# A ConvNeXt block with a gated head on one core: the first stage's ScalarE and VectorE order kept as written, centering products spread out, first image's GELUs placed behind evacuations

## The chip, the cores and the metric

The kernel runs on one core of one Trainium2 chip. The metric is the device time of one execution in microseconds (us). Engines are named as in the profile: PE is TensorE's matmul, PEld its weight load, DVE is VectorE, ACT is ScalarE, POOL is GpSimd, and SP is SyncE, which here only issues DMAs.

## The reference

The input x has 32 images of 384 channels and 28 x 28 pixels, in float32. One ConvNeXt-V2 block is followed by a gate on each image:

```python
y = conv7x7_depthwise(x)                      # 384 channels, padding 3
y = layernorm_over_channels(y) * ln_g + ln_b  # eps 1e-6
y = gelu(y @ w1 + b1)                         # 384 -> 1536
gx = sqrt(sum(y * y over the pixels))         # of each image and channel
y = grn_g * (y * gx / (mean(gx) + 1e-6)) + grn_b + y
y = x + (y @ w2 + b2)                         # 1536 -> 384, back to NCHW
# gate: mean, max and min over the pixels of y go through small matrices
out = sigmoid(logits[:, :, None, None] + y)
```

## The kernel before, in words

**The first stage** (0 to about 525 us) does the depthwise convolution and the layer norm's statistics for all images at once. It runs over NK = 48 steps `s` of TC = 8 channels, each step over 4 pairs `c2` of channels. `conv` makes three products of each channel with a banded matrix `tmat` (L661, L663, L665) into a PSUM bank `pc`. DVE then transposes the pair into `yt` (L668) and adds it to `acc` (L676), ACT squares it into `sq` (L681), and POOL adds two pairs' squares to `ssum` (L686). At the end of a step `yt` is stored to `yd`. Every 4 steps use one block `xt` of 32 channels. The next block is made meanwhile by `spread`: for each of 8 groups, `pad_x` copies an input tile into `xpad` (on ACT after the first block, L471), and `turn_x` transposes it on PE in two halves (L483) into a bank `pt`, which DVE (first half, L492) or ACT (second half, L494) copies into `xt`. The pad of group i+1 is issued at the first half of group i.

The weights are made in the same stage. `center_w` folds the layer norm's scale, shift and mean into w1 with small products (L566 into `pb`, L577 into `pm`) and three DVE updates for each `pm` (L583). `form_w` makes 15 combinations of w1 blocks (`UPSTEPS`, from step U1) and 38 of w2 blocks (`STEPS`, from step U2) for a fast matrix product. A form begins on POOL (L549) if two of its terms can be joined with a plain sum or difference, else on ACT (L552), and goes on on POOL (L555). Its tile `u` is one of three; the SP queue stores it to `u1d` or `u2d` at the end of the next step, after that step's `yd` store (L832).

The last two steps run in two halves of the images, so that the first image can be read back early. `first_image` adds the bias to it and makes its feature combinations (`forms_up`, L356). `finish` turns the sums into the factors of the layer norm, which go through DRAM (`rsd`) to `rb`.

**The second stage** runs image by image. `up(b)` is the first matrix product: two halves of 30 products each (L914) into banks A, B and C; ACT copies a bank (L921) or DVE adds it (L923 to L931). `down(b)` is the second one (L1042), whose operands POOL sums first (`sums`, L1003). Between them stand GELU (L879), the sum of squares (L890), `grn` (L938 to L950) and `scale` (L322, L324). For image 0 the layer norm's factor is multiplied after the product (`stretch`, L884, on POOL for the first six slices, on DVE and POOL in turn for the others). `within(b)` holds a table of hooks: `at((2, 4 * m), ...)` runs a function after product 4m of the second half of `up(b)`. The order of calls at the start is up(0), up(1), down(0), up(2), down(1), and so on.

**What sets the order on an engine.** The program is traced in Python, and a planner then orders each engine's instructions by its own estimate of when each is ready. `tc.keep_in_program_order(ins)`, here `keep`, ties an instruction to the earlier kept ones of its engine, so that these run as written; the others the planner may place before or after. Before the change, the conv products, the transposes on PE, and DVE's `L668` and `L676` are kept, and so are POOL's feature combinations and sums. Not kept are ACT's squares, pads, copies of `pt`, form copies, bank copies and GELUs, DVE's copies of `pt`, and the stretches.

Of the kernel before, what the change touches and what calls it, by code (L numbers as in the profile page):

```python
# [46 lines left out]
SQ = 4  # L47
# [150 lines left out]
def convnext_gate_kernel(  # L198
# [161 lines left out]
    with ExitStack() as one:  # L360
# [5 lines left out]
        psc = one.enter_context(tc.tile_pool(name="psc", bufs=5, space=bass.MemoryType.PSUM))  # L366
# [97 lines left out]

        def pad_x(i):
# [7 lines left out]
        keep = tc.keep_in_program_order  # L473

        def turn_x(i, h, xt, eng=nc.vector):
# [15 lines left out]
            if eng is nc.vector:  # L491
                eng.tensor_copy(dst, src)  # L492
            else:
                eng.activation(dst, src, AF.Identity)  # L494
# [8 lines left out]
        U1, U2 = 10, 23  # L503
# [38 lines left out]
        def form_w(name, wv, text, dst):  # L542
# [8 lines left out]
            else:  # L551
                nc.scalar.activation(t, blks[0][1], AF.Identity, scale=float(blks[0][0]))  # L552
# [5 lines left out]
        def center_w(part):  # L558

            if part == 0:  # L560
                nc.vector.tensor_copy(lr[:, :, 0], lnb_t)
                nc.vector.tensor_scalar(lr[:, :, 1], lng_t, -1.0 / C, None, ALU.mult)
                pb = psx.tile([P, 4, P], F32, tag="pt", name="pb").rearrange("p a b -> p (a b)")
                for f in range(FB):
                    for cb in range(CB):
                        nc.tensor.matmul(  # L566
                            pb[:, 2 * f : 2 * f + 2], w1r[:, cb, f * P : (f + 1) * P],
                            lr[:, cb], start=(cb == 0), stop=(cb == CB - 1),
                        )
                pbv = pb[:, : 2 * FB].rearrange("p (f v) -> p f v", v=2)  # L570
                nc.vector.tensor_tensor(b1f, pbv[:, :, 0], b1_t, ALU.add)
                nc.vector.tensor_copy(mcol, pbv[:, :, 1])
                return
            f0 = (part - 1) * 4
            pm = psx.tile([P, 4, P], F32, tag="pt", name=f"pm_{part}")
            for i in range(4):
                nc.tensor.matmul(  # L577
                    pm[:, i], mcol[:, f0 + i : f0 + i + 1].to_broadcast([P, P]), ident,
                    start=True, stop=True,
                )  # L580
            for cb in range(CB):
                w = w1r[:, cb, f0 * P : (f0 + 4) * P]
# [54 lines left out]
        def conv(s, c2, yt, xt, b0, b1):  # L637
# [42 lines left out]
            for ci in range(2):  # L680
                nc.scalar.activation(  # L681
                    part(sq)[:, cy % SQ + ci], part(pc[:, :, :N])[:, ci], AF.Square,
                    bias=dwb[:, cc + ci : cc + ci + 1], scale=1.0,
# [48 lines left out]
        def first_image(part):  # L732
# [4 lines left out]
            def raw(eng, cb, q0, q1):  # L737
# [5 lines left out]
                else:  # L743
                    eng.activation(d, src, AF.Identity, bias=dwb_t[:, cb : cb + 1], scale=1.0)
# [11 lines left out]
        for s in range(NK):  # L756
# [8 lines left out]
            if s in later:  # L765
# [3 lines left out]
                nc.gpsimd.tensor_copy(first, xpad[s % NPAD][: dst.shape[0], 0, :1])  # L769
# [6 lines left out]
            if s == NK - 1:  # L776
                y2 = yt, new_yt("yt_a1")
                first_image(0)
                for i in range(5):
# [26 lines left out]
                first_image(1)  # L806
# [70 lines left out]
    def gelu(b, f):  # L877
        y = ys[b][:, f, :]
        nc.scalar.activation(y, y, AF.Gelu, bias=b1f[:, f : f + 1], scale=1.0)  # L879

    def stretch(f, eng):

        y = ys[0][:, f, :].rearrange("p (r w) -> p r w", w=HW)
        eng.tensor_tensor(y, y, rows(rbs[0]), ALU.mult)  # L884
# [374 lines left out]
```

## Time and profile before

| | |
|---|---|
| median of 3 runs | 3081.61 us (3078.28 to 3082.94) |
| the profiled execution | 3081.39 us, its span 3079.6 us |
| busy share of the span | PE 98%, PEld 79%, DVE 64%, ACT 59%, POOL 79% |
| mean granted TensorE clock | 0.991 |
| first stage, PE | last conv product at about 525 us |
| up(0), first product of L914 | 527.6 us |

In the lines of the profile, `L681` is line 681 of the kernel. A line of the instructions in order of time has the start, the duration, the engine, the line and operation, out<-in with shapes, a count of instructions merged into it, and in brackets the idle time ahead of it and what ended that. A float32 product appears as two records. A line of busy time by stretch has the stretch, its length, then PE, PEld, DVE, ACT and POOL busy (with instructions), the granted clock, the DMA engines' share and GB/s. A line of waits has the waiting engine, its tile and line, then the one it waited for, and the total, the times and the longest.

### The profile page before, as it was taken

How to read it: one execution, taken by the hardware profiler on the slowest of the kernel's cores; microseconds unless marked ns; L12 is line 12 of the kernel's file. 1: busy time of each engine (PE TensorE's matmuls, PEld its weight loads, DVE VectorE, ACT ScalarE, POOL GpSimd, SP SyncE). 2: the span in 40 equal slices, each digit the busy share in tenths (PEclk: the TensorE clock that was granted, in tenths of full speed). 3: DMA queues.
4: the chain of work that ended last, by engine and by line, in shares of the span. 5: the costliest groups of instructions: out<-in, count | busy, mean ns of one | idle time of the engine just before them, and what ended most of it. 6: DMA issues, size and time to landing. Idle time of an engine off the chain costs nothing.

```text
span 3079.6 us, 44014 instructions
## 1 busy us (share of the span) xinstructions
PE 3013.7 (98%) x14435; PEld 2437.3 (79%) x14435; DVE 1985.0 (64%) x4555; ACT 1802.5 (59%) x3004; POOL 2438.4 (79%) x1829
## 2 busy tenths in 40 slices
PE   8999999899999999999999999999999999999998
PEld 7999988477777777777777777777777777777777
DVE  4555556656666666666666666666666666666666
ACT  4455554546666666666666666666666666666661
POOL 3356866398888888888888888888888888888897
PEclk9899999999999999999999999999999999999999
DMA  9799897456666666666666666666666666666546
GB/s 358 279 356 349 325 358 252 157 165 197 198 199 203 200 204 203 199 199 197 198 199 198 196 201 200 199 200 202 200 200 202 200 200 202 201 201 202 194 153 201
DMA packets 288475, 673.23 MB, mean 219 GB/s; under 512 B 31199, under 2 KB 111610, under 8 KB 282234
## 3 DMA queue, kind: packets, MB, share of 16 engines
q1 hardware_dynamic: 275156, 631.62, 62.4%
q10 hardware_dynamic: 13094, 38.80, 3.3%
q8 instruction: 118, 1.93, 0.3%
q14 instruction: 107, 0.88, 0.1%
HBM read 575.57 MB, written 94.76 MB: 218 GB/s over the span
## 4 chain that ended last, share of the span: by engine, by line
PE 87%; POOL 7%; DVE 3%; issue 1%; ACT 1%; DMA 1%; ACTq 0%; SPq 0%; DVEq 0%; POOLq 0%
PE ph_C L914 13%; PE ph_A L914 12%; PE ph_B L914 11%; PE pz_A L1042 7%; PE pz_C L1042 7%; PE pz_D L1042 7%; PE pz_F L1042 6%; PE pc L661 5%; PE pc L663 4%; PE pc L665 4%; POOL d_room L1003 3%; PE pt L483 2%; PE pz_H L1042 2%; PE pz_E L1042 2%; PE pz_I L1042 2%; DVE room L315 2%
## 5 line engine op out<-in xcount | busy, mean ns | idle before, releaser
L324 ACT ACTIVATE y<-y,fv,gsc 128x784 f32<-128x784 f32 x372 | 359.1, 1031 | 464.5 <-DVE gsc L950 464.5
L1003 POOL TENSOR_TENSOR d_room<-y 128x588 f32<-128x588 f32 x253 | 364.4, 1441 | 291.4 <-PE pz_B L1042 195.5
L879 ACT ACTIVATE y<-y,b1f 128x784 f32<-128x784 f32 x384 | 350.1, 945 | 230.5 <-DVE y L929 180.2
L914 PE MATMUL ph_A<-room,ws 128*128 128x392 f32 x1240 | 462.3, 495 | 10.6 <-ACT te L921 4.9
L914 PE MATMUL ph_C<-room,ws 128*128 128x392 f32 x1240 | 463.8, 496 | 5.3 <-DVE y L927 3.0
L914 PE MATMUL ph_B<-room,ws 128*128 128x392 f32 x1240 | 463.3, 496 | 5.7 <-ACT y L921 3.5
L1003 POOL TENSOR_TENSOR d_room<-d_room,y 128x588 f32<-128x588 f32 x308 | 440.9, 1436 | 16.8
L914 PEld LDWEIGHTS ph_C<-room,ws 128*128 128x128 f32 x1240 | 234.4, 191 | 190.4 <-DVE y L927 28.6
L914 PEld LDWEIGHTS ph_A<-room,ws 128*128 128x128 f32 x1240 | 236.2, 191 | 185.7 <-ACT te L921 5.6
L914 PEld LDWEIGHTS ph_B<-room,ws 128*128 128x128 f32 x1240 | 236.2, 191 | 171.9 <-ACT y L921 4.6
L890 ACT ACTIVATE junk<-y 128x784 f32<-128x784 f32 x384 | 329.0, 857 | 8.9
L1003 POOL TENSOR_TENSOR d_room<-y,d_room 128x588 f32<-128x588 f32 x214 | 306.2, 1437 | 26.9 <-PE pz_D L1042 15.8
L686 POOL TENSOR_TENSOR ssum<-ssum,sq 128x896 f32<-128x896 f32 (+1 forms) x100 | 201.7, 2017 | 150.6 <-ACT sq L681 148.7
L356 POOL TENSOR_TENSOR room<-room 128x392 f32<-128x392 f32 x303 | 303.5, 1018 | 11.9
L1003 POOL TENSOR_TENSOR y<-y 128x588 f32<-128x588 f32 x180 | 258.7, 1437 | 7.1
L925 DVE TENSOR_TENSOR y<-y,ph_B 128x392 f32<-128x392 f32 x256 | 137.5, 556 | 167.2 <-ACT y L879 123.5
L923 DVE TENSOR_TENSOR y<-y,ph_C 128x392 f32<-128x392 f32 x384 | 212.1, 560 | 26.3 <-PE ph_C L914 1.6
L661 PE MATMUL pc<-xt,tmat 128*128 128x224 f32 x736 | 203.5, 358 | 15.4 <-ACT sq L681 10.1
L1042 PE MATMUL pz_A<-d_room,u 128*128 128x196 f32 x1050 | 202.9, 329 | 0.1
L1042 PEld LDWEIGHTS pz_A<-d_room,u 128*128 128x128 f32 x1050 | 178.8, 190 | 7.7 <-POOL d_room L1003 0.4
L663 PE MATMUL pc<-xt,tmat 128*96 128x192 f32 x736 | 181.7, 329 | 0.0
L665 PE MATMUL pc<-xt,tmat 128*128 128x192 f32 x736 | 181.2, 328 | 0.0
(265 smaller groups left out, 6258.4 us busy)
## 6 DMA issues: line engine op xcount, KB each, us to landing
u<-u2d SPq DMA_DIRECT2D x487, 384.0 KB, 3.8
ws<-u1d SPq DMA_DIRECT2D x384, 320.0 KB, 3.0
tmat<-fs SPq DMA_DIRECT2D x47, 1420.0 KB, 10.5
ws<-u2d SPq DMA_DIRECT2D x121, 384.0 KB, 3.8
yi<-yd SPq DMA_DIRECT2D x95, 448.0 KB, 6.2
yd<-yt SPq DMA_DIRECT2D x46, 896.0 KB, 9.3
x<-in_x SPq DMA_DIRECT2D x32, 1176.0 KB, 5.6
out<-x ACTq DMA_DIRECT2D x31, 1176.0 KB, 9.4
```

Of the source, the lines that this page charges most:

```text
L324: eng.activation(out, in_, AF.Identity, bias=add, scale=mul)
L356: tc.keep_in_program_order(eng.tensor_tensor(d, o[in0], o[in1], op))
L661: keep(nc.tensor.matmul(po, t[:, c, P : 2 * P], xc, start=True, stop=False))
L663: nc.tensor.matmul(lo, t[:, c, 2 * P : T0 + MW], after, start=False, stop=False)
L665: keep(nc.tensor.matmul(hi, t[:, c, :P], before, start=False, stop=True))
L686: nc.gpsimd.tensor_tensor(part(ssum), part(ssum), part(sq), ALU.add)
L879: nc.scalar.activation(y, y, AF.Gelu, bias=b1f[:, f : f + 1], scale=1.0)
L890: nc.scalar.activation(junk, ys[b][:, f, :], AF.Square, accum_out=ssqs[b][:, f : f + 1])
L914: nc.tensor.matmul(banks[t, bk][:, :NH], wts[t][:, i % UG, :], o[opnd], start=(first == 1), stop=True, skip_group_check=True,)
L923: nc.vector.tensor_tensor(d, d, p, ALU.add)
L1003: nc.gpsimd.tensor_tensor(d[0], o[a][0], o[c][0], ALU.add if sign == "+" else ALU.subtract)
L1042: nc.tensor.matmul(pz[:, :NQ4], wt[:, i % UD, t, :], o[opnd][0][:, t, :], start=(first and t == 0), stop=(t == KD - 1), skip_group_check=True,
```

## The change

There are six edits. On ACT and DVE, every instruction of the first stage's loop is now kept: pads, copies of `pt`, squares, form copies, and the first image's bias on ACT. The centering products are no longer made in blocks at the ends of steps 7, 8 and 9; one or two groups follow each pair's conv products in steps 7 to 10, in a PSUM bank of their own (`psb`), and `psc` has four banks instead of five. U1 goes from 10 to 11, the forms of w1 are spread over 9 steps at 3/5 steps each, and those of w2 end one step earlier. `first_image` is in three parts, the first two at the ends of steps 44 and 45 instead of at the start of the last step. POOL's small copies that hold back a load until its step read `acc` instead of `xpad`. In the second stage, image 0's GELUs, squares and stretches and the bank copies of images 0 and 1 are kept, and some hooks move.

```diff
-        psc = one.enter_context(tc.tile_pool(name="psc", bufs=5, space=bass.MemoryType.PSUM))
+        psb = one.enter_context(tc.tile_pool(name="psb", bufs=1, space=bass.MemoryType.PSUM))
+        psc = one.enter_context(tc.tile_pool(name="psc", bufs=4, space=bass.MemoryType.PSUM))
...
             if i < NG:
                 nc.gpsimd.tensor_copy(dst, src)
             else:
-                nc.scalar.activation(dst, src, AF.Identity)
+                keep(nc.scalar.activation(dst, src, AF.Identity))
...
             if eng is nc.vector:
-                eng.tensor_copy(dst, src)
+                keep(eng.tensor_copy(dst, src))
             else:
-                eng.activation(dst, src, AF.Identity)
+                keep(eng.activation(dst, src, AF.Identity))
...
-        U1, U2 = 10, 23
+        U1, U2 = 11, 23
...
-                nc.scalar.activation(t, blks[0][1], AF.Identity, scale=float(blks[0][0]))
+                keep(nc.scalar.activation(t, blks[0][1], AF.Identity, scale=float(blks[0][0])))
...
+        def center_w(n):
+
+            if n < FB:
+                if n == 0:
...
+                    cent["pb"] = psb.tile([P, 4, P], F32, tag="pb", name="pb").rearrange(
+                        "p a b -> p (a b)"
+                    )
+                pb = cent["pb"]
+                for cb in range(CB):
+                    keep(
                         nc.tensor.matmul(
-                            pb[:, 2 * f : 2 * f + 2], w1r[:, cb, f * P : (f + 1) * P],
+                            pb[:, 2 * n : 2 * n + 2], w1r[:, cb, n * P : (n + 1) * P],
                             lr[:, cb], start=(cb == 0), stop=(cb == CB - 1),
                         )
...
+            f = n - FB
+            if f % 4 == 0:
+                cent["pm"] = psb.tile([P, 4, P], F32, tag="pb", name=f"pm_{f}")
+            pm = cent["pm"]
+            keep(
                 nc.tensor.matmul(
-                    pm[:, i], mcol[:, f0 + i : f0 + i + 1].to_broadcast([P, P]), ident,
+                    pm[:, f % 4], mcol[:, f : f + 1].to_broadcast([P, P]), ident,
                     start=True, stop=True,
                 )
+            )
+            if f % 4 < 3:
+                return
             for cb in range(CB):
...
             for ci in range(2):
-                nc.scalar.activation(
-                    part(sq)[:, cy % SQ + ci], part(pc[:, :, :N])[:, ci], AF.Square,
-                    bias=dwb[:, cc + ci : cc + ci + 1], scale=1.0,
+                keep(
+                    nc.scalar.activation(
+                        part(sq)[:, cy % SQ + ci], part(pc[:, :, :N])[:, ci], AF.Square,
+                        bias=dwb[:, cc + ci : cc + ci + 1], scale=1.0,
+                    )
                 )
...
                 raw(nc.scalar, 0, 0, NQD)
                 raw(nc.scalar, 1, 0, NQD)
+            elif part == 1:
                 forms_up(0, nc.gpsimd, early=True)
...
-                nc.gpsimd.tensor_copy(first, xpad[s % NPAD][: dst.shape[0], 0, :1])
+                nc.gpsimd.tensor_copy(first, acc[: dst.shape[0], 0, :1])
...
-                first_image(0)
-                for i in range(5):
+                for i in range(4):
...
-                first_image(1)
+                first_image(2)
...
                     conv(s, c2, yt, xt, 0, B)
+                    q = (s - U1 + 4) * PAIRS + c2
+                    if 0 <= q < 4 * PAIRS:
+                        for n in range(q * 3 // 2, (q + 1) * 3 // 2):
+                            center_w(n)
                     if k + 1 < NX:
                         spread(k + 1, si * PAIRS + c2, xn)
...
+                if NK - 4 <= s:
+                    first_image(s - NK + 4)
...
-            if U1 - 3 <= s < U1:
-                for part in ((0,), (1,), (2, 3))[s - U1 + 3]:
-                    center_w(part)
...
-                if s != U1 + i * 2 // 3:
+                if s != U1 + i * 3 // 5:
...
-                if s != U2 + i * (NK - 2 - U2) // ND:
+                if s != U2 + i * (NK - 3 - U2) // ND:
...
-        nc.scalar.activation(y, y, AF.Gelu, bias=b1f[:, f : f + 1], scale=1.0)
+        ins = nc.scalar.activation(y, y, AF.Gelu, bias=b1f[:, f : f + 1], scale=1.0)
+        if b == 0:
+            tc.keep_in_program_order(ins)
...
-        eng.tensor_tensor(y, y, rows(rbs[0]), ALU.mult)
+        tc.keep_in_program_order(eng.tensor_tensor(y, y, rows(rbs[0]), ALU.mult))
...
-                            nc.scalar.activation(d, p, AF.Identity)
+                            ins = nc.scalar.activation(d, p, AF.Identity)
+                            if b < 2:
+                                tc.keep_in_program_order(ins)
...
-                at((0, 24), normed, 1)
-                at((2, 0), forms_up, 1)
+                at((0, 20), normed, 1)
+                at((0, 24), forms_up, 1)
...
-                at((0, 2 + 2 * m), gelu, p, HF + m)
-                at((0, 14 + m), square, p, HF + m)
-            at((0, 20), grn, p)
+                at((0, 6 + 2 * m), gelu, p, HF + m)
+                at((0, 17 + m), square, p, HF + m)
+            at((0, 23), grn, p)
             for i, f in enumerate(order):
-                at((0, 22) if i < 6 else (2, 0), scale, p, f, V if i % 3 else A)
-            at((0, 23), sums, p)
+                at((0, 24) if i < 6 else (2, 0), scale, p, f, V if i % 3 else A)
+            at((0, 26), sums, p)
...
-                at((2, 2 + 4 * m), gelu, b, m)
+                at((2, (2 if b else 8) + 4 * m), gelu, b, m)
             for m in range(squared(b)):
-                at((2, 28 if m >= HF // 2 else 22 + 2 * m), square, b, m)
+                at((2, 29 if m >= HF // 2 or not b else 22 + 2 * m), square, b, m)
```

More of the change, by code (lines that the diff above doesn't have):

```diff
@@ L463, in load_x @@
             )
+        keep = tc.keep_in_program_order
         def pad_x(i):
@@ L470, in pad_x @@
             else:
-                nc.scalar.activation(dst, src, AF.Identity)
-        keep = tc.keep_in_program_order
+                keep(nc.scalar.activation(dst, src, AF.Identity))
         def turn_x(i, h, xt, eng=nc.vector):
@@ L556, in form_w @@
             stores.append((dst, t))
[L558 to L565, printed above, removed]
+        cent = {}
+        def center_w(n):
+            if n < FB:
+                if n == 0:
+                    nc.vector.tensor_copy(lr[:, :, 0], lnb_t)
+                    nc.vector.tensor_scalar(lr[:, :, 1], lng_t, -1.0 / C, None, ALU.mult)
+                    cent["pb"] = psb.tile([P, 4, P], F32, tag="pb", name="pb").rearrange(
[4 more added lines that the diff above has]
+                    keep(
@@ L566, in center_w @@
                         nc.tensor.matmul(
-                            pb[:, 2 * f : 2 * f + 2], w1r[:, cb, f * P : (f + 1) * P],
+                            pb[:, 2 * n : 2 * n + 2], w1r[:, cb, n * P : (n + 1) * P],
                             lr[:, cb], start=(cb == 0), stop=(cb == CB - 1),
                         )
-                pbv = pb[:, : 2 * FB].rearrange("p (f v) -> p f v", v=2)
-                nc.vector.tensor_tensor(b1f, pbv[:, :, 0], b1_t, ALU.add)
-                nc.vector.tensor_copy(mcol, pbv[:, :, 1])
@@ L573, in center_w @@
-                return
-            f0 = (part - 1) * 4
-            pm = psx.tile([P, 4, P], F32, tag="pt", name=f"pm_{part}")
-            for i in range(4):
+                    )
+                if n == FB - 1:
+                    pbv = pb[:, : 2 * FB].rearrange("p (f v) -> p f v", v=2)
+                    nc.vector.tensor_tensor(b1f, pbv[:, :, 0], b1_t, ALU.add)
+                    nc.vector.tensor_copy(mcol, pbv[:, :, 1])
+                return
+            f = n - FB
+            if f % 4 == 0:
+                cent["pm"] = psb.tile([P, 4, P], F32, tag="pb", name=f"pm_{f}")
@@ L577, in center_w @@
+            pm = cent["pm"]
+            keep(
                 nc.tensor.matmul(
-                    pm[:, i], mcol[:, f0 + i : f0 + i + 1].to_broadcast([P, P]), ident,
+                    pm[:, f % 4], mcol[:, f : f + 1].to_broadcast([P, P]), ident,
                     start=True, stop=True,
                 )
+            )
+            if f % 4 < 3:
+                return
             for cb in range(CB):
-                w = w1r[:, cb, f0 * P : (f0 + 4) * P]
+                w = w1r[:, cb, (f - 3) * P : (f + 1) * P]
@@ L680, in conv @@
             for ci in range(2):
-                nc.scalar.activation(
-                    part(sq)[:, cy % SQ + ci], part(pc[:, :, :N])[:, ci], AF.Square,
-                    bias=dwb[:, cc + ci : cc + ci + 1], scale=1.0,
+                keep(
+                    nc.scalar.activation(
+                        part(sq)[:, cy % SQ + ci], part(pc[:, :, :N])[:, ci], AF.Square,
+                        bias=dwb[:, cc + ci : cc + ci + 1], scale=1.0,
+                    )
                 )
@@ L743, in raw @@
                 else:
-                    eng.activation(d, src, AF.Identity, bias=dwb_t[:, cb : cb + 1], scale=1.0)
+                    keep(
+                        eng.activation(d, src, AF.Identity, bias=dwb_t[:, cb : cb + 1], scale=1.0)
+                    )
             if part == 0:
@@ L889, in square @@
         junk = junkp.tile([P, NT], F32, tag="junk", name=f"junk_{b}_{f}")
-        nc.scalar.activation(junk, ys[b][:, f, :], AF.Square, accum_out=ssqs[b][:, f : f + 1])
+        ins = nc.scalar.activation(
+            junk, ys[b][:, f, :], AF.Square, accum_out=ssqs[b][:, f : f + 1]
+        )
+        if b == 0:
+            tc.keep_in_program_order(ins)
     def up(b, hooks):
@@ L920, in up @@
                         if how == "copy":
-                            nc.scalar.activation(d, p, AF.Identity)
+                            ins = nc.scalar.activation(d, p, AF.Identity)
+                            if b < 2:
+                                tc.keep_in_program_order(ins)
                         elif how == "add":
```

## The prediction

> **What bounds the kernel now.** I read the page first: TensorE (PE) is busy 98% of the span, so a gain must come from PE's gaps, from slow-clock time or from PE work removed. The chain that ended last gives PE 87% and POOL only 7%. From about 700 us on the slices show PE and its clock at 9 tenths or more; the change reaches nothing there. So I asked for busy time by stretch, then the list of waits, then the instructions in order of time, for the first 720 us only.
>
> The waits of 50 to 500 us (engine, line, what it waited for: us, times, longest) hold one entry for PE, and those of 0 to 620 us say who is late:
> ```profile
> PE pc L661 <- ACT sq L681: 10.1, 7, 2.7
> ...
> ACT xt L494 <- PE pt L483: 181.3, 84, 17.4
> POOL ssum L686 <- ACT sq L681: 148.7, 62, 6.2
> ```
> PE lacks a free conv bank 7 times. ScalarE (ACT) meanwhile stands 84 times on a transpose that PE has yet to make, with older squares queued behind it. One such place, in order of time:
> ```profile
> 433.12 0.95 ACT L744 ACTIVATE room<-yi,cv 128x784 f32<-128x784 f32 x1
> 433.98 0.51 ACT L552 ACTIVATE u<-ws 128x384 f32<-128x384 f32 x1
> ...
> 434.35 0.69 DVE L492 COPY xt<-pt 128x512 f32<-128x512 f32 x1 [4.19 <-PE pt L483]
> 434.96 0.64 DVE L668 STREAM_TRANSPOSE yt<-pc 128x448 f32<-128x448 f32 x1
> ...
> 436.20 0.79 ACT L681 ACTIVATE sq<-pc,dwb 128x224 f32<-128x224 f32 x2 [1.71 <-DVE acc L676]
> ...
> 437.04 0.65 PE L661 MATMUL pc<-xt,tmat 128*128 128x224 f32 x2 [2.72 <-ACT sq L681]
> ```
> VectorE (DVE) waits 4.19 us for the newest transpose while finished conv pairs lie unread, then drains six in a row.
>
> The centering products form one block (start, duration, engine), and the two stretches after it give PE busy, other engines, granted clock, DMA share:
> ```profile
> 105.68 13.01 PE L566 MATMUL pb<-lr,ws 128*128 128x2 f32 x72
> ...
> 110.00:115.00 5.00, 5.00 (x25) 5.00 (x25) 0.00 (x0) 0.00 (x0) 0.00 (x0) 0.50 1.03 415
> 115.00:120.00 5.00, 5.00 (x22) 4.84 (x22) 0.25 (x2) 0.00 (x0) 0.00 (x0) 0.50 0.78 293
> ```
> The clock falls to 0.50 although PE counts as busy. Between the stages:
> ```profile
> 555.86 0.95 ACT L879 ACTIVATE y<-y,b1f 128x784 f32<-128x784 f32 x1 [11.04 <-POOL y L884]
> 556.72 0.86 ACT L921 ACTIVATE y<-ph_B 128x392 f32<-128x392 f32 x2
> ...
> 587.83 1.79 ACT L879 ACTIVATE y<-y,b1f 128x784 f32<-128x784 f32 x2 [6.64 <-POOL y L884]
> ...
> 557.25 1.58 PE L914 MATMUL ph_B<-room,ws 128*128 128x392 f32 x4 [3.52 <-ACT y L921]
> ...
> 563.76 2.98 PE L914 MATMUL ph_A<-room,ws 128*128 128x392 f32 x4 [3.61 <-ACT y L921]
> ...
> 576.84 2.98 PE L914 MATMUL ph_A<-room,ws 128*128 128x392 f32 x4 [4.94 <-ACT te L921]
> ```
> A GELU waits for POOL's stretch of y, and the bank copies behind it hold PE three times.
>
> [...] the copy at 556.72 starts when the GELU ends. [...] here stores of u1d from 163 to 235 us take
> ```profile
> DMA to landing us min/median/max: 4.0/5.8/6.6
> ```
> while several u2d stores from 330 to 410 us take 8.8 to 13.6.
>
> **The change, part by part.** The sum is made against the profiled execution: 3081.39 us, span 3079.6, 1.8 around it; the median of the runs shown, 3081.61, is 0.2 higher.
>
> (a) *Order as written.* Squares and reads of a pair now come before newer transposes. PE's waits for banks go: 10.1 us. [...] 77.4 to 81.3 us ran at 0.56, so 3.9 x 0.44 = 1.7 back. What is late next: a pair takes PE 2.06 us, DVE 0.63 + 0.58 and ACT 0.78 after it, so four banks instead of five (8 us) still cover. The bounds of this part are 6 and 12.
>
> (b) *Centering spread.* At full clock 24 records took 2.3 us (105.7 to 108), 0.096 each; 72 make 6.9 instead of 12.9: 6.0 saved. The conv work behind it (118.6 to 121.8) ran at 0.50: 1.6 more. The 24 records of pm cost about 0.11 each in both forms. Sum 7.6; if half clock came back at every group it would be 0.
>
> (c) *The single bank psb.* Each pm group of four must be read by three DVE operations of 0.74 us (the row of L583) before the next group's first product[...]. By the step numbers, products 19 and 20 fall in one pair: PE waits for DVE's 1.2 us of conv reads and 2.2 of updates, 3.4 us. Products 15 and 16 are one pair apart, so 2.06 + 0.2 are covered: 1.1. Loss 4.5, bounds 0 and 7.
>
> (d) *Stage end.* The last forms come one step earlier, the early features two. Today POOL has them at 505 to 515 us, the squares wait for ssum, and PE stands 1.7 us and then runs 517.3 to 521.3 at 0.57 (1.7). Gain 3.4, bounds 0 and 4. The SP queue, which waited 6.0 us there for POOL's last form, frees its stores of yt earlier.
>
> (e) *form_w's ScalarE copies kept.* This adds the wait that no trace of before shows. Three u buffers rotate. Where the form three earlier was made one step earlier, its store is issued only after the current step's yd store, directly before the new copy; ACT now stands until that store lands. With 22 steps for 38 forms this holds for forms 3, 5, 10, 12, 17, 22, 24, 29, 31, 36; those starting on ACT are 3, 22, 29, 31, 36 (steps 24, 35, 39, 40, 43). Queued behind: the next pair's squares and the next pad copy, which PE's transposes need. From the end of a step's last conv: store issued at 1.15, landing 5.9, copy 0.5, squares 0.75, pad 0.85: 9.15. After steps 35 and 39 the new channel block needs that pad at 4.9 (two pairs and seven transposes), so PE stands 4.25, and the clock drops for 1.7; step 35 also issues two yi loads ahead of the store, 1.2 more. 7.1 + 5.9. After 24 and 40 two more squares and one evacuation go first, 10.25 against 9.35: 0.9 each. After 43 no pads remain and four banks cover it. Sum 14.8, taken as 15; bounds 0 (stores issued or landed sooner) and 45 (landing 11).
>
> (f) *GELUs behind evacuations.* Count from the first ph_B product, T = 527.6. The rb load for image 1 lands at T+18, its normed parts end at T+23; then POOL does ten forms of 1.02 us, now wholly ahead of six stretches of 1.86: stretches end at T+44, as today (T+45). GELU 0 now sits eight products into the second half, so only products 18 on wait: PE ends up(0) near T+46 instead of T+60. ACT then has GELUs to T+45, six squares (1.03 each) to T+51, six bank copies to T+54. The 6.64 us that ACT stood before 587.83 close, and grn comes that much earlier. From grn on POOL's sums (39 of 1.43 us and ten forms) bind until about 680 us, so PE's 14 us shrink to 6.6. Bounds 0 (DVE held by normed, which moves four products earlier than its data) and 12.
>
> (g) *At nothing*: the tiny POOL copies now read acc; DVE's next add may wait some 1.6 us for ssum ahead of the copy, covered by four banks. U1 one step later: POOL is busy 38 of 50 us at most before 500.
>
> Sum: 10.1 + 1.7 + 7.6 + 3.4 - 4.5 - 15 + 6.6 = 9.9 saved; 3081.4 - 9.9 = **3071.5 us**.
>
> **The rivals.**
> *1. The copies of (e) hardly wait* (3 us in all): stores land early in a smoother stream. For it: with nothing bunched the queue should drain, and 1.8 us landings occur near 494. Against it: DMA share is 0.99 at full pace. 22.8 - 3 - 4.5 + 6.6 = 21.9: 3059.5.
> *2. Slower.* The same copies at steps 24, 35, 39, 40 and 43 wait for stores landing after 9 us. By the working of (e): 10.2 + 9.1 + 2 x 5.7 + 3.2 = 34 us lost, so 3081.4 + 34 + 4.5 - 22.8 - 6.6 = 3090.5. It decides from a landing of about 7.5 us on. For it: 8.8 to 13.6 in the second half of the stage. Against it: those fall where the SP queue stood up to 12 us on late forms and then issued everything at once.
> *3. The stage between brings nothing*: POOL's order, forms first, or normed at the head of DVE keeps grn where it is. 3078.
> *4. The order is not what limits*: 16 DMA engines at 0.93 to 1.00 share take PE's saved time back as waits for tmat or room. Then (a) is lost: 3083. Against it: 163 to 235 us ran PE without a gap at share 0.99.
>
> **How the numbers follow.** Forecast 0.42, rival 1 0.25, rival 2 0.16, rival 3 0.10, rival 4 0.07. A difference of 0.2%, 6.2 us, is about what a measurement of this kernel can tell from no change. Faster takes most of the forecast and rival 1: 0.67; same 0.15; slower 0.18. The range runs from rival 1 with its transition at 12 and psb near 0 (3048) to rival 2 (3090).
>
> **What would show it.** Right: PE's waits for ACT sq under 2 us; no clock of 0.50 near 110 us; up(1)'s first product some 10 us nearer to up(0)'s; grn 5 us or more nearer. In (e), ACT u L552 waiting for DMA u2d, and PE pt waiting for ACT xpad at five places after step 23. Wrong: no such waits (rival 1), over 25 us of them (rival 2), or PE waiting for DMA (rival 4).

## The result and the profile after

The kernel became slower. The median is 3092.64 us (3089.71 to 3097.09, 5 runs), against 3079.62 us (3076.89 to 3082.94, 5 runs) for the kernel before on the same chip: ratio 1.0044, 95% interval 1.0029 to 1.0058, so 13 us lost where 9.9 were to be saved. The profiled execution took 3089.71 us, its span 3087.7 us (before: 3079.6).

The first product of up(0) starts at 543.20 us instead of 527.63, 15.6 later, and the span is only 8.1 longer: the first stage lost 15.6, and the stretch behind it won 7.5 back. So the question is about the first stage. Its waits from 50 to 500 us (engine, line, what it waited for: us, times, longest):

```profile
PE pt L484 <- ACT xpad L474: 22.0, 5, 8.8
...
POOL u L550 <- DMA u2d<-u: 11.5, 3, 6.2
...
ACT u L553 <- DMA u2d<-u: 9.2, 1, 9.2
DVE yt L682 <- DMA yd<-yt: 8.9, 2, 7.2
ACT u L553 <- DMA yd<-yt: 7.3, 1, 7.3
...
PE pm L588 <- DVE ws L597: 3.8, 2, 3.1
...
DVE acc L690 <- POOL ws L788: 2.8, 1, 2.8
```

The bank wait of before (PE pc on ACT sq, 10.1 us, 7 times) is gone, and of ACT's waits for newer transposes (72 in this stretch of the kernel before) one of 1.8 us is left. In their place PE stands on *pads*, 22.0 us in five waits. The other lines say what ACT's pads were queued behind: store landings and POOL's small copy.

**A ledger by step.** Four steps share a block of 32 channels, and the PE work of a step depends on its place among the four alone: an undisturbed one takes 10.20, 10.09, 9.77 or 9.00 us (values that recur in all the traces). The start of each step can be read from the instructions in order of time, since each has 16 records of its first conv product. What a step takes beyond those values is its loss, idle and half clock together. The loss of steps 1 to 44, us to the rounding (step 44, which has no transposes, is counted from its own value, 8.23), with the start of up(0) and the span:

| kernel | step 4 | 7 to 10 (centering) | 20 | 25 to 28 | 36 | others | sum | up(0) | span |
|---|---|---|---|---|---|---|---|---|---|
| before | 0.0 | 17.6 | 0.4 | 0.0 | 0.0 | 14.0 | 31.9 | 527.6 | 3079.6 |
| after | 9.0 | 16.4 | 5.0 | 6.1 | 11.9 | 4.3 | 52.6 | 543.2 | 3087.7 |

So the 14.0 us that before lost in single places (4.0 in step 5, 3.0 in 23, 3.0 in 39, 1.9 in 40, the rest in small pieces) are gone, and some 32 us came at four new ones. The first of them, in order of time:

```profile
64.87 0.49 PE L679 MATMUL pc<-xt,tmat 128*128 128x192 f32 x2
68.86 0.65 DVE L682 STREAM_TRANSPOSE yt<-pc 128x448 f32<-128x448 f32 x1 [7.19 <-DMA yd<-yt]
...
70.11 0.78 ACT L696 ACTIVATE sq<-pc,dwb 128x224 f32<-128x224 f32 x2 [7.56 <-DVE acc L690]
...
70.78 0.85 ACT L474 ACTIVATE xpad<-room 128x784 f32<-128x784 f32 x1
...
71.69 1.11 PE L484 MATMUL pt<-ident,xpad 128*128 128x128 f32 x4 [6.33 <-ACT xpad L474]
```

DVE cannot write `yt` because the store of that buffer, issued at the end of step 2 behind the load of w1 (2304 KB), has not landed (issued at 52.62 us, landed at 68.77); the run with w1 in three parts, below, tests this. ACT's squares wait for DVE, the pad is written behind the squares, and PE's transposes need the pad. The four transposes then take 1.11 us instead of 0.60: the granted clock is 0.50 from 69.95 to 76.77 us. The planner of the kernel before met the same load like this:

```profile
62.88 0.65 DVE L668 STREAM_TRANSPOSE yt<-pc 128x448 f32<-128x448 f32 x1 [0.90 <-PE pc L665]
...
65.86 0.69 DVE L492 COPY xt<-pt 128x512 f32<-128x512 f32 x1 [1.82 <-PE pt L483]
...
68.20 0.69 DVE L492 COPY xt<-pt 128x512 f32<-128x512 f32 x1 [1.65 <-PE pt L483]
...
73.69 0.64 DVE L668 STREAM_TRANSPOSE yt<-pc 128x448 f32<-128x448 f32 x1
...
77.43 1.05 PE L661 MATMUL pc<-xt,tmat 128*128 128x224 f32 x2 [2.00 <-ACT sq L681]
```

Between two conv transposes lie nearly 11 us in which DVE went on with the next block's copies and ACT with its pads; the store landed meanwhile, and PE lost 4.0 us in step 5. What looked like bunching in the profile before was also what hid late stores.

Two more of the places, a form copy at the end of step 35 and the small copy of step 20:

```profile
423.88 0.52 ACT L553 ACTIVATE u<-ws 128x384 f32<-128x384 f32 x1 [9.18 <-DMA u2d<-u]
424.31 0.77 ACT L696 ACTIVATE sq<-pc,dwb 128x224 f32<-128x224 f32 x2
424.97 0.85 ACT L474 ACTIVATE xpad<-room 128x784 f32<-128x784 f32 x1
...
425.88 1.11 PE L484 MATMUL pt<-ident,xpad 128*128 128x128 f32 x4 [8.78 <-ACT xpad L474]
```

```profile
248.76 0.18 POOL L788 COPY ws<-acc 128x1 f32<-128x1 f32 x1
248.98 0.62 DVE L690 TENSOR_TENSOR acc<-acc,pc 128x448 f32<-128x448 f32 x1 [2.76 <-POOL ws L788]
249.69 0.78 ACT L696 ACTIVATE sq<-pc,dwb 128x224 f32<-128x224 f32 x2 [4.15 <-DVE acc L690]
...
251.28 1.11 PE L484 MATMUL pt<-ident,xpad 128*128 128x128 f32 x4 [2.93 <-ACT xpad L474]
```

The form copy waits as the prediction said, for a store that takes 8.9 us to land. In the other, POOL makes its copy behind a form of w1, DVE's next add into `acc` must wait for POOL, then the same chain follows. The fourth place, the form copy at the end of step 24, waited 7.3 us for a `yd` store (the line ACT u on DMA yd above).

In the second stage, the lines that answer to the three waits of before at 557, 563 and 576 us are

```profile
553.66 2.04 PE L941 MATMUL ph_B<-room,ws 128*128 128x392 f32 x4 [4.33 <-ACT y L948]
...
563.37 1.58 PE L941 MATMUL ph_C<-room,ws 128*128 128x392 f32 x4 [3.80 <-DVE y L952]
```

and the second half runs on without such a wait.

### The profile page after: what moved, and what is told of

Its sections match the earlier page's. It is cut to its first block, busy times and chain, and to the rows that moved or that the text cites. A ratio compares the mean times of both kernels' runs of the same rounds, so it can differ in the third digit from the quotient of the medians.

```text
span 3087.7 us, 44113 instructions
## 1 busy us (share of the span) xinstructions
PE 3011.4 (98%) x14435; PEld 2434.4 (79%) x14435; DVE 1994.1 (65%) x4554; ACT 1808.4 (59%) x3004; POOL 2438.7 (79%) x1829
## 4 chain that ended last, share of the span: by engine, by line
PE 86%; DVE 5%; POOL 4%; DMA 2%; ACT 1%; issue 1%; SPq 0%; DVEq 0%; ACTq 0%; POOLq 0%
PE ph_C L941 14%; PE ph_A L941 12%; PE ph_B L941 11%; PE pz_A L1071 8%; PE pz_C L1071 8%; PE pz_F L1071 7%; PE pz_D L1071 7%; PE pc L675 4%; PE pc L679 3%; PE pc L677 3%; PE pz_H L1071 2%; PE pz_I L1071 2%; PE pz_E L1071 2%; PE pt L484 2%; DVE room L315 2%
## 5 line engine op out<-in xcount | busy, mean ns | idle before, releaser
L1032 POOL TENSOR_TENSOR d_room<-d_room,y 128x588 f32<-128x588 f32 x308 | 440.7, 1435 | 16.8
L356 POOL TENSOR_TENSOR room<-room 128x392 f32<-128x392 f32 x303 | 303.4, 1018 | 11.9
L696 ACT ACTIVATE sq<-pc,dwb 128x224 f32<-128x224 f32 x368 | 144.5, 444 | 227.0 <-DVE acc L690 211.4
L682 DVE STREAM_TRANSPOSE yt<-pc 128x448 f32<-128x448 f32 x184 | 119.5, 649 | 208.3 <-PE pc L679 194.9
```

What stands on the lines that cost most here:

```text
L356: tc.keep_in_program_order(eng.tensor_tensor(d, o[in0], o[in1], op))
L696: nc.scalar.activation(part(sq)[:, cy % SQ + ci], part(pc[:, :, :N])[:, ci], AF.Square, bias=dwb[:, cc + ci : cc + ci + 1], scale=1.0,)
L1032: nc.gpsimd.tensor_tensor(d[0], o[a][0], o[c][0], ALU.add if sign == "+" else ALU.subtract)
```

## The experiments

The theory: the order as written ties the pads, which feed PE's transposes, to every landing and every POOL copy that a square, a DVE transpose or a form copy waits for; and half clock follows some of PE's waits (0.50 behind the 6.33 us above). The rivals: the DMA rate is the limit, or the centering in its single bank and the four conv banks cost it. The ledger for all experiments:

| kernel | step 4 | 7 to 10 | 20 | 25 to 28 | 36 | others | sum | up(0) | span |
|---|---|---|---|---|---|---|---|---|---|
| four u buffers | 7.6 | 16.4 | 1.9 | 0.6 | 0.3 | 4.7 | 31.4 | 525.7 | 3072.5 |
| yt in halves | 4.2 | 16.4 | 7.1 | 2.3 | 10.0 | 5.2 | 45.2 | 540.5 | 3085.2 |
| pads first | 5.3 | 16.3 | 0.4 | 1.1 | 9.1 | 0.1 | 32.2 | 524.9 | 3073.9 |
| second stage alone | 0.0 | 17.6 | 0.4 | 0.0 | 0.0 | 16.8 | 34.8 | 526.8 | 3067.6 |
| four edits | 0.0 | 17.5 | 0.4 | 0.0 | 0.0 | 0.1 | 17.9 | 515.3 | 3062.6 |
| four edits, block | 0.6 | 16.1 | 0.4 | 0.0 | 0.0 | 0.1 | 17.1 | 511.9 | 3062.3 |
| small copies | 7.6 | 16.4 | 0.7 | 5.3 | 10.7 | 4.2 | 44.8 | 537.8 | 3085.9 |
| form copy free | 9.3 | 14.7 | 3.0 | 5.3 | 10.7 | 5.4 | 48.4 | 539.2 | 3087.0 |
| order alone | 7.6 | 16.2 | 0.7 | 5.8 | 0.3 | 20.7 | 51.3 | 543.9 | 3093.0 |
| four edits, spaced | 0.1 | 10.4 | 0.4 | 0.0 | 0.0 | 0.1 | 10.9 | 505.8 | 3052.9 |
| w1 in three | 3.9 | 16.4 | 4.8 | 6.2 | 11.9 | 4.0 | 47.2 | 541.1 | 3092.6 |
| spaced, planner's order | 2.9 | 10.4 | 0.4 | 0.0 | 0.0 | 7.0 | 20.6 | 513.4 | 3061.6 |

Ahead of step 1 all of these start 1.0 to 4.0 us later than the kernel after did in its profiled execution, before anything of the change has run. So sums are compared, not only up(0).

**Four u buffers**

```diff
-        dwb = tp.tile([P, C], F32, name="dwb")
+        dwb = room[:, 7 * NT : 7 * NT + C]
-        ufp = one.enter_context(tc.tile_pool(name="ufp", bufs=3))
+        ufp = one.enter_context(tc.tile_pool(name="ufp", bufs=4))
```

> The kernel after with four u buffers instead of three (room for the fourth comes from putting dwb at the end of the tile room). Theory (the written order ties ACT's pads and squares to a store's landing): the waits of ACT's form copy, 7.31 us at 308 and 9.18 us at 424, go, with the PE waits behind them and the half clock that follows (about 4.3 + 1.0 and 11.8 us by the starts of the steps): span about 17 us shorter, near 3071 in the profiled execution and 3076 in the median. The waits at 68 and 249 us stay. Rival (the DMA queue's rate is the limit, the copies only show it): the loss moves to waits for yd, tmat or room, and less than 4 us come back, 3088 or more. Second rival (centering and four conv banks cost it): no change within 3 us.

Measured: 3072.47 us, ratio to the kernel before 0.9979 (0.9969 to 0.9988). The sum falls by 21.2 us: 17.1 of it in steps 25 to 28 and 36, as said, and 4.5 in steps 4 and 20, which was not expected. One more buffer of 2 KB per partition turns a loss against before into a gain. This speaks against the DMA rival: the same bytes moved.

**yt in halves**

```diff
+                    if c2 % 2:
+                        cy = s * TC + 2 * c2 - 2
+                        nc.sync.dma_start(yd[:, cy : cy + 4, :], yt[c2 // 2])
...
-                nc.sync.dma_start(yd[:, s * TC : (s + 1) * TC, :], yt)
```

> The kernel after, where yt is kept in halves: four buffers of 4 channels instead of two of 8, and each half is stored as soon as its two pairs are transposed, so that the first half's store is issued two pairs (about 4 us) earlier. Same bytes, twice as many stores. Theory: DVE's wait for the store at 61 to 69 us (7.19) shrinks by about 4 us for the first half, PE's 6.33 us wait for the pad behind it shrinks to about 2 and the clock does not fall: some 6 to 8 us back, and part of the 7.31 us of the form copy at 308, which waited for a yd store: span 8 to 12 us shorter, near 3078. Rival (the DMA rate is the limit): with the same bytes queued ahead, the halves land no earlier in sum, and the loss stays: within 2 us of the kernel after.

Measured: 3087.79 us, ratio 1.0032 (1.0023 to 1.0042). At its two places it did what it should: step 4 lost 4.2 instead of 9.0, DVE's wait there is 3.15 instead of 7.19, and steps 25 to 28 lost 2.3 instead of 6.1. PE's wait behind it is 2.30 us, and half clock followed all the same (two records of L677 took 0.85 us at 70.39, 0.49 at 65.23), which the expectation had excluded. Some 3 us came back as new losses, in steps 20 and 40 above all, so a gain of 7.4 us is left in the sum and of 2.5 in the span: the total was missed, the places were right.

**Pads first**

```diff
+                turn_x(i, h, xn, (nc.vector, nc.scalar)[h])
+
+        def pads(k, q):
+            for n in plan[q]:
+                g, h = divmod(n, 2)
                 if h == 0:
-                    pad_next(i + 1)
-                turn_x(i, h, xn, (nc.vector, nc.scalar)[h])
+                    pad_next(k * NG + g + 1)
...
                 for c2 in range(PAIRS):
+                    if k + 1 < NX:
+                        pads(k + 1, si * PAIRS + c2)
                     conv(s, c2, yt, xt, 0, B)
```

> The kernel after, where each pair's pad is issued (and kept) ahead of that pair's conv products and squares instead of behind them; everything else as written. Theory: pads no longer queue behind squares that wait for DVE: the 0.28 us lost twice in each block of four steps go (about 6 us over the stage), and of the 10 us at 62 to 72 most go, since the pad does not stand behind DVE's wait any more; the form copies at the ends of steps 24 and 35 still stand ahead of the next pads, so 300 to 311 and 414 to 432 keep their losses: 12 to 15 us shorter, near 3075. Rival (place in the queue is not what costs, DMA or banks are): within 3 us of the kernel after.

Measured: 3073.80 us, ratio 0.9984 (0.9977 to 0.9990). The sum falls by 20.4. The 0.27 us that the kernel after loses twice in most blocks are gone (others 4.3 to 0.1), and step 20 is clean. Steps 25 to 28, which were to keep their loss, fell from 6.1 to 1.1 as well; step 36 kept 9.1. Step 4 kept 5.3, for a reason that the expectation did not have:

```profile
70.41 0.65 DVE L682 STREAM_TRANSPOSE yt<-pc 128x448 f32<-128x448 f32 x1 [7.76 <-DMA yd<-yt]
...
71.49 0.68 DVE L493 COPY xt<-pt 128x512 f32<-128x512 f32 x1
...
72.22 0.82 PE L484 MATMUL pt<-ident,xpad 128*128 128x128 f32 x3 [3.39 <-DVE xt L493]
```

The pads went on, but DVE's copies of `pt` are kept too, behind the transpose that waits: PE ran out of `pt` banks. Each engine's written order has its own chain.

**The second stage alone** (the first stage as in the kernel before, with the edits of the second stage, in the diff all those from the GELUs on)

> The kernel before up to the end of the first stage, with the second-stage edits alone (kept GELUs, squares, stretches, bank copies, moved hooks). Theory: up(0) starts as in the kernel before, near 527.6 us, and the stretch to about 680 us is 6 to 8 us shorter: 3073 in the profiled execution. Rival (the transition has slack of its own, and the kernel after only lost less because its first stage ended late while loads and POOL's features went on): less than 2 us, 3079 to 3082.

Measured: 3070.00 us, ratio 0.9977 (0.9971 to 0.9984), 7 to 8 us gained; in the profiled execution the span is 12.0 shorter, of which 0.9 lie ahead of up(0), and up(1) starts 49.8 us after up(0) (before: 60.1). Part (f) of the change is a gain by itself.

**The four edits together** (the three above, and the small copies on xpad again)

> The kernel after with four edits together: four u buffers, pads ahead of their pair's conv products, yt in halves of 4 channels stored at once, POOL's small copies reading xpad again instead of acc. Theory (each loss of the kernel after is a place in ACT's or DVE's written order that waits for a landing or for POOL): they nearly add up. Four u buffers gave 17.5 us at the start of up(0) (3 of them ahead of step 1), pads first 6 over the stage, the halves 4 at step 4, the small copies 2 to 4 at step 20: up(0) starts at 512 to 516 us, span 3057 to 3062. Rival (the DMA rate takes it back once PE is faster): up(0) not before 522, span 3068 or more, with PE waits for tmat, xt or room in place of xpad.

Measured: 3063.49 us, ratio 0.9948 (0.9933 to 0.9963). Of the 36.3 us that the kernel after lost outside the centering, 0.4 remain. This decides against the DMA rate: with 34.7 us less time for the same bytes, PE waits nowhere for tmat, room or xt between 50 and 500 us.

**The same with the centering in blocks and five conv banks**

> The same four edits, and the centering as in the kernel before: blocks at the ends of three steps (8, 9, 10 with U1 at 11), products in psx banks, no bank psb, and five conv banks. Against the run with four edits alone this is the worth of the spread centering with four banks. The prediction had 7.6 - 4.5 = 3.1 us gained by the spread; the trace of the kernel after shows 1.2 at steps 7 to 10. So up(0) is 1 to 3 us later than with the four edits alone. Rival (four banks and the single psb bank cost more than the spread brings): earlier by 2 us or more.

Measured: 3064.11 us, ratio 0.9953 (0.9937 to 0.9970). Neither side: the same within what can be told, 16.1 us of centering against 17.5. The spread centering, as the change has it, brings nothing here.

**The small copies alone**

```diff
-                nc.gpsimd.tensor_copy(first, acc[: dst.shape[0], 0, :1])
+                nc.gpsimd.tensor_copy(first, xpad[s % NPAD][: dst.shape[0], 0, :1])
```

> The kernel after with one edit: POOL's small copies that hold back a load read xpad, as in the kernel before, instead of acc. Theory: DVE's wait of 2.76 us at 249 us and PE's 2.93 behind it, with the half clock from 251.3 to 254.7, go: step 20 is 4.6 us shorter, the rest as in the kernel after. Rival (POOL's or ACT's queue there holds PE anyway): step 20 keeps 3 us or more of its 15.3, since the pad behind the squares waits for something else.

Measured: 3089.22 us, ratio 1.0032 (1.0019 to 1.0045). Step 20 lost 0.7 instead of 5.0: 4.3 us for one copy of one element per partition. The interval overlaps that of the kernel after, so the size rests on the trace.

**The form copy not kept**

```diff
-                keep(nc.scalar.activation(t, blks[0][1], AF.Identity, scale=float(blks[0][0])))
+                nc.scalar.activation(t, blks[0][1], AF.Identity, scale=float(blks[0][0]))
```

> The kernel after with one edit: ACT's form copies are not kept, so the planner may place them behind pads and squares; buffers and stores are unchanged. Theory: the copy moves behind a part of the later pads and squares, the losses at 300 to 311 (5.3) and at 414 to 432 (11.8) go for the most part: 12 to 17 us shorter at the start of up(0). Rival (the planner's own due times place the copy at the same point, ahead of the pads, since it does not count on a late landing): less than 3 us.

Measured: 3090.31 us, ratio 1.0035 (1.0022 to 1.0048). The rival was right: the planner puts the copy at the same point, and it waits as long. Steps 25 to 28 and 36 lost 2.0 us less together, not 12 to 17. (Another 1.7 of the lower sum lie in the centering, where the same wait of PE, 3.09 us, was not followed by half clock this time: two records of L677 took 0.49 us at 149.76, where the kernel after has 0.85 at 150.03.)

```profile
420.59 0.52 ACT L553 ACTIVATE u<-ws 128x384 f32<-128x384 f32 x1 [9.15 <-DMA u2d<-u]
421.68 0.85 ACT L474 ACTIVATE xpad<-room 128x784 f32<-128x784 f32 x1
...
422.58 1.12 PE L484 MATMUL pt<-ident,xpad 128*128 128x128 f32 x4 [8.34 <-ACT xpad L474]
```

So it is not that the copy is kept that costs; the pads and squares behind it are kept too, and can no longer go ahead.

**The order alone**, on the kernel before

```diff
-                nc.scalar.activation(dst, src, AF.Identity)
+                keep(nc.scalar.activation(dst, src, AF.Identity))
...
-                eng.tensor_copy(dst, src)
+                keep(eng.tensor_copy(dst, src))
...
-                nc.scalar.activation(
-                    part(sq)[:, cy % SQ + ci], part(pc[:, :, :N])[:, ci], AF.Square,
-                    bias=dwb[:, cc + ci : cc + ci + 1], scale=1.0,
+                keep(
+                    nc.scalar.activation(
+                        part(sq)[:, cy % SQ + ci], part(pc[:, :, :N])[:, ci], AF.Square,
+                        bias=dwb[:, cc + ci : cc + ci + 1], scale=1.0,
+                    )
                 )
```

> The kernel before with one edit: ACT's pads, both copies of pt and the squares are kept in the order written (form copies, centering, U1, small copies, image 0's part and the second stage stay as before). This is part (a) of the prediction alone. The prediction's step: 11.8 us gained, span 3068. Theory now: the order as written puts pads behind squares, and so behind every wait of DVE and ACT for a landing. The kernel before lost about 14 us in steps 1 to 44 outside the centering, the kernel after about 37, of which 4.4 belong to the small copies reading acc. So steps 1 to 44 become 10 to 17 us longer, with PE waits for xpad near steps 4, 25 and 36: span 3088 to 3096. Rival (only the kept form copies and the small copies cost): gained, 3068 to 3072.

Measured: 3095.74 us, ratio 1.0050 (1.0033 to 1.0066): slower by 15 us. Its waits from 50 to 500 us:

```profile
ACT u L552 <- DMA u2d<-u: 22.1, 9, 7.2
PE pt L483 <- ACT xpad L473: 21.1, 7, 5.5
...
ACT u L552 <- DMA yd<-yt: 7.5, 1, 7.5
```

The form copies, not kept here, wait ten times for landings of `u2d` and `yd`, and the pads behind them hold PE seven times. The kernel before has neither entry for ACT in the same stretch. Outside the centering it lost 35.0 us by the ledger where the kernel before lost 14.4. One part of the change thus costs as much as the whole lost; and since this kernel has five conv banks and the centering in blocks, neither of these is the cause.

**The four edits with spaced centering groups**

```diff
-                        for n in range(q * 3 // 2, (q + 1) * 3 // 2):
+                        now = range(q * 3 // 2, (q + 1) * 3 // 2)
+                        if q >= 8:
+                            now = ((12,), (13, 14), (15,), (), (16, 17), (18, 19), (), (20, 21, 22, 23))[q - 8]
+                        for n in now:
```

> The run with four edits together, and the centering's last three groups of four products spaced so that two pairs of conv products lie between the last product of a group and the first of the next (the single bank psb and all else as there). Theory (the bank psb holds PE, part (c) of the prediction, and the stall of 3.1 us also halves the clock): PE pm's waits of 3.8 us go and with them 1.7 to 3 us of half clock at step 10: 5 to 7 us shorter than the run with four edits, up(0) that much earlier, span near 3057. Rival (the products themselves cost it, their number times their length): within 1 us.

Measured: 3055.58 us, ratio 0.9917 (0.9902 to 0.9932), 25 us faster than the kernel before and the best of all. Steps 9 and 10 lost 2.7 instead of 9.8: 7.1 us, a little more than said; some 3 of them are half clock, two stretches of 3.41 us with the four edits (0.50 from 143 to 146 us) and none here (two records of L677 take 0.49 us all through steps 9 and 10). The busy time by stretch (stretch, length, PE, PEld, DVE, ACT, POOL busy, granted clock, DMA share, GB/s) of the kernel after and then of this one:

```profile
50.00:100.00 50.00, 43.62 (x260) 41.55 (x259) 25.49 (x44) 22.86 (x51) 18.89 (x11) 0.93 0.98 354
400.00:450.00 50.00, 41.17 (x243) 39.17 (x242) 23.01 (x40) 22.81 (x52) 25.56 (x17) 0.90 0.88 316
```

```profile
50.00:100.00 50.00, 50.00 (x324) 48.49 (x323) 28.54 (x52) 26.40 (x61) 21.43 (x14) 1.00 0.99 358
400.00:450.00 50.00, 50.00 (x320) 48.55 (x319) 30.48 (x53) 30.24 (x68) 37.79 (x28) 1.00 0.92 344
```

PE has no gap, at full clock, with the DMA share no lower than in the kernel after. And DVE still waits for a store at the same place, without cost:

```profile
67.10 0.65 DVE L682 STREAM_TRANSPOSE yt<-pc 128x448 f32<-128x448 f32 x1 [4.25 <-DMA yd<-yt]
68.37 0.79 ACT L696 ACTIVATE sq<-pc,room 128x224 f32<-128x224 f32 x2 [3.89 <-DVE acc L690]
```

Four banks covered this wait of 4.25 us, with no pad behind it.

**w1 loaded in three**, at steps 2, 3 and 5

```diff
-            2: (
-                ws.rearrange("p (cb f) -> p cb f", f=FF),
-                w1.rearrange("(cb p) f -> p cb f", p=P),
-            ),
+            **{
+                (2, 3, 5)[cb]: (
+                    ws.rearrange("p (cb f) -> p cb f", f=FF)[:, cb : cb + 1],
+                    w1.rearrange("(cb p) f -> p cb f", p=P)[:, cb : cb + 1],
+                )
+                for cb in range(CB)
+            },
```

> The kernel after with one edit: the load of w1 (2304 KB at step 2) is made in three of 768 KB, at steps 2, 3 and 5. Theory (the yd store that DVE waits for at 61 to 69 us lies in the queue behind w1): the wait of 7.19 us and the pad's 6.33 behind it shrink to under 3 us, step 4 loses 2 us or less instead of 7.6 to 10; later steps as in the kernel after; up(0) 6 to 9 us earlier, span 3079 to 3082. Rival (the DMA rate, 0.96 to 1.0 share there whatever the order): the loss is spread over steps 4 to 6 and stays within 2 us.

Measured: 3087.36 us, ratio 1.0027 (1.0017 to 1.0037). Between the two: step 4 loses 3.9 us instead of 9.0, the later steps are as in the kernel after, and DVE's wait is 2.86 instead of 7.19:

```profile
67.04 0.65 DVE L685 STREAM_TRANSPOSE yt<-pc 128x448 f32<-128x448 f32 x1 [2.86 <-DMA yd<-yt]
```

So the store was held up by the load of w1 issued ahead of it: from the store's issue to DVE's transpose it took 16.24 us in the kernel after (52.62 to 68.86), and 12.38 here (54.66 to 67.04), by the split alone. In this profiled execution (the slowest of its ten) the second stage took 7.0 us longer than in that of the kernel after; why stays open.

**The spaced version in the planner's order** (no pad, copy of `pt`, square or form copy of the first stage kept)

> The run with four edits and spaced groups, with none of the first stage's pads, copies of pt, squares and form copies kept (the planner orders them as in the kernel before; conv's DVE operations, the products and the second stage stay kept). It asks what the written order is worth once the buffers are there. Theory (the kernel before lost 16 us outside the centering to the planner's order of ACT and DVE: steps 5, 23, 35, 38, 39): most of these come back, steps 1 to 44 are 8 to 16 us longer than with the order kept, span 3061 to 3068. Rival (buffers and spacing alone did it, the order is worth nothing by itself): within 3 us of the kept version, span 3053 to 3056.

Measured: 3062.65 us, ratio 0.9944 (0.9927 to 0.9960); the sum is 9.7 above the kept version, and the bank waits are back (PE pc on ACT sq, 7.1 us, 4 times). So the written order is worth about 9 us of span, once the buffers carry it.

## Why the prediction was wrong

The prediction's terms beside what the profiled pair and the runs showed (gains positive, us):

| part | predicted | measured | from |
|---|---|---|---|
| (a) bank waits and clock of before | +11.8 | +14.0 | others, 14.0 in before |
| (a) "what is late next" | 0 | -13.3 | step 4 (9.0), pads behind squares (others, 4.3) |
| (b) centering spread | +7.6 | +7.1 | 17.6 to 10.4 in the spaced version |
| (c) single bank psb | -4.5 | -5.9 | 16.4 in after against 10.4 |
| (d) stage end | +3.4 | +2.0 | step 45 starts 17.6 later, up(0) 15.6 |
| (e) form copies | -15 | -17.9 | steps 25 to 28 and 36 |
| (f) transition | +6.6 | +7.5 | up(0) to the end |
| (g) at nothing | 0 | -4.6 | step 20 |
| ahead of step 1 | 0 | +3.0 | not of the change |
| sum | +9.9 | -8.1 | span |

The medians differ by 13.0 and the spans by 8.1: the profiled execution of after is the fastest of its five, and it came to step 1 at 30.8 us, earlier than the profile of any other kernel here (31.8 to 34.8). The table explains that one execution, not the median.

**The step that failed is (a), "What is late next".** It listed one pair's work on PE, DVE and ACT (2.06, 0.63 + 0.58, 0.78) and concluded that four banks of 8 us still cover. That is true of the banks: PE did not wait for one on ACT sq before the last two steps, and a DVE wait of 4.25 us cost nothing in the spaced version. But PE needs a second thing from ACT, the pad. Written behind the pair's squares, it comes one pair ahead of its transposes at best, so the long waits of DVE and ACT went to PE (7.19 us of DVE became 6.33 of PE, 9.18 of ACT became 8.78). In before the pads ran ahead and hid the landings. The kept order alone lost 19.4 us by the ledger, where +11.8 stood. The prediction had seen this very chain, and used it in (e) alone, for the copies. It asked who waits for the instruction behind, but only for the wait that it knew to be new, not for the waits that were already in the trace (DVE yt on DMA yd) and that the old order had covered.

**(g) failed for the same reason.** The wait of DVE's add on POOL's copy was foreseen (1.6 us; it took 2.76) and put at nothing under the cover of the banks. The pad had no such cover: 2.93 us of PE, then 3.4 us at a clock of 0.56. The small-copies run put 4.3 us on it.

**(e) was right in mechanism and near in size**, 17.9 for 15, but not in its places: of the five named, steps 24 and 35 lost 6.1 and 11.9 (predicted 0.9 and 7.1), and those at 39, 40 and 43 nothing, where 6.8 were counted. At step 35 the landing took 8.9 us, not 5.9. Rival 2 gave nearly the right time, and two of its five waits came near its prices (6.1 and 11.9 against 5.7 and 10.2); the other three, 18 us of its sum, did not come, and other losses, (a) and (g), stood in their place, so that its time was near by luck. And the wait does not hang on the copy being kept, as the free form copy shows, but on what is kept behind it.

**(b) and (c)** were right in sign and near in size. The half clock near 110 us is gone (1.00 there in after), and 7.1 of 7.6 us came, but the single bank took 5.9 of them: its waits were 3.8 us (4.5 in the prediction), and half clock behind the longer one, 3.09 us (0.50 from 148.45 to 151.87), which the prediction left out, made up the rest. The change as written gained 1.2.

**(d)** brought 2.0 of 3.4. PE still waited for the last features:

```profile
543.20 1.77 PE L941 MATMUL ph_B<-room,ws 128*128 128x392 f32 x4 [2.49 <-DVE room L356]
```

**(f)** was right in size. Of its signs, up(1) came 7.5 us nearer to up(0) (60.1 to 52.6, "some 10"), but grn of image 0 did not move (76.1 to 75.9 us after the start of up(0)); that of image 1 came 4.6 earlier. Alone, behind the first stage of before, the same edits brought up(1) 10.4 us nearer and grn of image 0 3.0. Rival 3 is excluded by the run with the second stage alone. Rivals 1 and 4 fall with (e) and with the four edits.

## What to carry to other kernels

When an order is fixed by hand, list for each engine everything that another engine needs from it, and for each kept instruction the latest landing or foreign copy that anything ahead of it may wait for; a product that feeds the bound engine (here the pad) goes ahead of work that can wait (here the squares). Waits that cost nothing in the old trace are part of that list, since the old order may have been what hid them. Fix the order and deepen the buffers together: here the order alone lost 15 us, the order with a fourth u buffer, halved stores, pads first and spaced groups gained 25, and the same buffers without the order gained 18 (some 7 of each from the second stage).

## What the runs showed of the hardware

Whether a wait of PE halved the clock did not go by its length. In the kernel before, a wait of 2.00 us (at 75.4) was followed by half clock, and two of 2.72 us (at 273.7 and 434.3) were not; one of 3.48 us in the run with the form copy free was not either. The traces show what went with it. In each of them all changes of the clock lie a whole number of intervals of 3.41 us apart, and what went with half clock was how much of one such interval PE stood idle. Below are, first for the kernel before and then for the form copy free, three intervals each in order of time (the PE busy time comes after the length, the clock stands third from the end):

```profile
74.09:77.50 3.41, 1.41 (x10) 1.12 (x9) 3.41 (x8) 2.03 (x5) 0.18 (x1) 1.00 1.05 442
77.50:80.92 3.42, 3.42 (x10) 3.10 (x11) 0.52 (x2) 1.90 (x6) 2.65 (x2) 0.50 1.09 242
80.92:84.33 3.41, 3.41 (x24) 3.31 (x24) 2.42 (x5) 0.03 (x1) 1.50 (x1) 1.00 0.69 62
```

```profile
304.04:307.45 3.41, 1.56 (x10) 1.24 (x8) 1.53 (x3) 1.42 (x4) 1.09 (x2) 1.00 1.05 420
307.45:310.87 3.42, 1.78 (x13) 1.75 (x14) 0.69 (x1) 3.42 (x10) 3.01 (x2) 1.00 0.60 170
310.87:314.28 3.41, 3.41 (x23) 3.31 (x22) 1.76 (x3) 1.87 (x5) 2.09 (x1) 1.00 0.89 343
```

The wait of 2.00 us lay within one interval; that of 3.48 was shared out, 1.85 and 1.64. Over the fourteen traces, from 30 to 3040 us, each of the 85 full-clock intervals with 2.00 us or more of idle PE was followed by half clock (5 of them in the kernel before, 8 in the kernel after); of the 118 with 0.90 to 1.99 us, 6 were (all with 1.56 or more, one of them in the kernel before, 1.72 us from 514.4; why these, is not shown). So the same wait of 3.09 us for the single bank was followed by one such interval at half clock in the kernel after, by two with the four edits and by none with the form copy free (steps 7 to 10: 16.4, 17.5 and 14.7 us). An estimate from these: a wait with half clock behind it costs its length and, for each interval, up to 1.7 us (3.41 x 0.5). The kernel after, just behind its wait of 2.93 us:

```profile
251.30:254.70 3.40, 3.40 (x13) 3.21 (x14) 0.69 (x1) 1.72 (x4) 3.40 (x3) 0.56 1.07 407
```

2-column products (L566), whose block ran at half clock though PE counted as busy (0.50 from 110 to 120 us in the kernel before), ran at 1.00 when put between conv products (100 to 125 us in the kernel after), 6 to 12 records at a time, at about 0.11 us a record. Four such blocks, in four of the traces, are the only places where half clock followed an interval with less than 0.9 us of idle PE.
